# Weight loads in two parts, asked for right behind the split that frees their buffer

## Chip, cores and metric

The kernel runs on one core of one Trainium2 chip. The metric is the device time of one execution in microseconds (us). Before the change it is 750.67 us, the median of three runs (748.7 to 752.8 us).

## What is computed

For each of 1024 samples there are 32 fields of 128 numbers. For each of the 496 pairs of fields (i, j) with i < j there is a weight matrix of 128 x 128. The output of a pair is field i times its matrix, multiplied element by element with field j:

```python
v_i = inputs[:, I_IDX, :]
v_j = inputs[:, J_IDX, :]
transformed = jnp.einsum('bpd,ped->bpe', v_i, W)
return transformed * v_j
```

The output is 1024 x 496 x 128 floats, 260 MB, and has to be written to HBM; the weights are 32.5 MB and the fields 16.8 MB.

## The kernel before

**Pairs and units.** The pairs are taken in the order of falling i: field 30 with 31 first, field 0 with 1 to 31 last. Number q counts pairs (0 to 495); each pair has two units u = 2q and 2q + 1, one for each half of the 1024 samples. The program is one loop over u, in which every engine's instructions are written down in the order in which that engine takes them; nothing is reordered afterwards (`manual_schedule`).

**A unit.** `first(u)` (line 202) issues two matmuls on PE (L212: xh with wh, xl with wl) into one PSUM bank and lets ACT multiply the bank by 1 + 2^-12 (L213). `second`, three units later, issues the third matmul (L221: xd with wd), then DVE multiplies the bank with field j into an output tile (L227). An output tile holds four pairs (2 MB). ACT issues its store (L258). The first 15 pairs use one plain fp32 matmul instead (L209).

**Splits.** Three fast matmuls stand for one exact one, so weights and fields are split into three parts first. `split_w` takes two pairs of weights: ACT makes wh (L127), POOL wl and wd (L128, L129, L130). `split_x` takes half of a field: ACT makes xh (L142), POOL xl (L143, L144), and xd is made by POOL (L148) for fields 0 to 9 and by DVE (L265) for the others. The splits stand in a list `todo`, ordered by the pair that needs them; at the odd units the loop takes one that may start. A split of weights may start five pairs ahead of its use, one of field i at the start of field i + 1's block of pairs.

**Weight loads.** Weights come in 62 chunks of eight pairs (512 KB) into a ring of three buffers (`rpool`). Field 0's load (`x_0`) takes one turn in the same ring, between chunks 54 and 55. A chunk may be loaded once the last of its four splits has read the chunk that had the buffer before. `w_at` says at which pair each load is issued: for chunk c at pair 8c - 17, for chunks 55 to 57 at pair 8c - 11.

**Loads in two parts.** The even chunks from 12 to 60 (`WAPART`, 25 of them) are loaded by `load_apart`: POOL issues 112 rows (448 KB, L102) and SP the other 16 (64 KB, L103). All other chunks are one load of SP (L118). Three pairs behind such a load (`BACK`) POOL issues a tiny DMA into a scratch tile, `move_on` (L99), which moves on the round in which POOL's DMAs take the DMA engines.

**Other loads.** Fields 1 to 16 come in four group loads of 2 MB (`load_group`, L108, tiles x_g), issued by SP at pairs 52, 141, 219 and 313 (`XAT`). Their space holds output tiles until 20 pairs before that, so the number of output buffers falls from seven to three in the course of the run.

**Queues.** POOL takes its splits and its DMA issues in one order; a DMA issue takes its time in that order. SP does nothing but issue loads, in the order of the program, and stands still at one whose buffer is not free yet. ACT's stores stand among its splits and multiplies.

Of the kernel before, what the change touches and what calls it, by code (L numbers as in the profile page):

```python
# [13 lines left out]
NQ = NF * (NF - 1) // 2  # L14
BT = 1024
HB = 512
WC = 2
WL = 8
# [6 lines left out]
WB = 3  # L25
WLEAD = 12
XAFTER = 54
# [3 lines left out]
NE = 14  # L31
ROWS = 8 * NE
WAPART = tuple(range(12, 62, 2))
BACK = 3
# [11 lines left out]
def kernel(  # L46
# [35 lines left out]
    def load_x(f, pieces=1, eng=None):  # L82
        if f == 0:

            t = rpool.tile([P, WL, P], F32, tag="w", name="x_0").rearrange("p q e -> p (q e)")
        else:
            t = xpool.tile([P, BT], F32, tag=f"x{f}", name=f"x_{f}")
        s = BT // pieces
        for k in range(pieces):
            (eng or nc.sync).dma_start(out=t[:, k * s : (k + 1) * s], in_=xt[f, :, k * s : (k + 1) * s])  # L90
        x_sb[f] = t
# [5 lines left out]
    def move_on(k):  # L97

        nc.gpsimd.dma_start(out=mark[: 2 * k], in_=xt[0, : 2 * k, :16].rearrange("(b a) n -> a b n", a=k))  # L99

    def load_apart(dst, src):
        nc.gpsimd.dma_start(out=dst[:ROWS], in_=src[:ROWS].rearrange("(b a) m n -> a b m n", a=NE))  # L102
        nc.sync.dma_start(out=dst[ROWS:], in_=src[ROWS:])  # L103

    def load_group(k):
        t = xpool.tile([P, XG, BT], F32, tag=f"g{k}", name=f"x_g{k}")
        f = XG * k + 1
        nc.sync.dma_start(out=t, in_=xt[f : f + XG].rearrange("m d b -> (m d b)").rearrange("(d m b) -> d m b", m=XG, b=BT))  # L108
        for m in range(XG):
            x_sb[f + m] = t[:, m, :]  # L110

    def load_w(c, splits=(0, WL), eng=nc.sync):
        w_raw[c] = rpool.tile([P, WL, P], F32, tag="w", name=f"w_{c}")
        if c in WAPART:
            load_apart(w_raw[c], wt[c])
            return
        for a, b in zip(splits, splits[1:]):
            eng.dma_start(out=w_raw[c][:, a:b, :], in_=wt[c, :, a:b, :])  # L118

    w_s = {}  # L120

    def split_w(c, u):

        k = c * WC % WL
        raw = w_raw[c * WC // WL][:, k : k + WC, :].rearrange("p q e -> p (q e)")
        h, l, d = [wpool.tile([P, WC * P], F32R, tag=t, name=f"{t}_{c}") for t in ("wh", "wl", "wd")]
        nc.scalar.mul(h, raw, 1.0 - 2.0**-13)  # L127
        nc.gpsimd.tensor_tensor(l, raw, h.bitcast(F32), ALU.subtract)  # L128
        nc.gpsimd.tensor_scalar(d, h.bitcast(F32), EPS, 1.0, ALU.mult, ALU.mult)  # L129
        nc.gpsimd.tensor_tensor(d, l.bitcast(F32), d.bitcast(F32), ALU.subtract)  # L130
        w_s[c] = (h, l, d)

    x_s = {}
    later = []
# [22 lines left out]
    for c in range(c0, nchunk):  # L157
        todo.append(((c - 3) * WC + 1, max(c * WC, nq0), lambda u, c=c: split_w(c, u)))
# [16 lines left out]
    w_at = {}  # L175
    for c in range(WB, -(-NQ // WL)):
        free = (c - WB + 1) * WL if (c - WB) * WL < nq0 else 0
        early = 0 if XAFTER < c <= XAFTER + WB else WLEAD - 6
        w_at[max(c * WL - 3 * WC - 5 - early, free)] = c
    x_at = XAFTER * WL - 11  # L180
    assert x_at not in w_at and len(w_at) == NQ // WL - WB

    w_q = {c: q for q, c in w_at.items()}
    back = []

    ngroup = NF // XG // 2
    group_at = {q: k for k, q in enumerate(XAT)}
# [14 lines left out]
    def first(u):  # L202
        q, h = divmod(u, 2)
        i, c = pairs[q][0], q // WC
        r = slice(q % WC * P, (q % WC + 1) * P)
        s = slice(h * HB, (h + 1) * HB)
        po[u] = ppool.tile([P, HB], F32, tag="po", name=f"po_{u}")
        if q < nq0:
            nc.tensor.matmul(po[u], w_raw[q // WL][:, q % WL, :], x_sb[i][:, s], start=True, stop=True)  # L209
        else:  # L210
            for t in (0, 1):
                nc.tensor.matmul(po[u], w_s[c][t][:, r], x_s[i][t][:, s], start=t == 0, stop=t == 1)  # L212
            nc.scalar.mul(po[u], po[u], 1.0 + EPS)  # L213

    def second(u):
        q, h = divmod(u, 2)
        i, j = pairs[q]
        r = slice(q % WC * P, (q % WC + 1) * P)
        s = slice(h * HB, (h + 1) * HB)
        if q >= nq0:  # L220
            nc.tensor.matmul(  # L221
                po[u], w_s[q // WC][2][:, r], x_s[i][2][:, s], start=False, stop=True, skip_group_check=True
            )
        g, k = divmod(q, OG)
        if k == 0 and h == 0:
            ots[g] = out_tile(g)
        nc.vector.tensor_tensor(ots[g][:, k, s], po.pop(u), x_sb[j][:, s], ALU.mult)  # L227
        if q >= NQ - 2:
            stores.append((u + SLAG, out[g, :, k, s], ots[g][:, k, s]))
        elif g == 0 or q >= NQ - OG:  # L230
            if h == 1:
                stores.append((u + SLAG, out[g, :, k], ots[g][:, k]))
        elif k == OG - 1 and h == 1:
            stores.append((u + SLAG, out[g], ots[g]))

    for u in range(2 * NQ + LAG + SLAG):
        q = u // 2
        if u < 2 * NQ:
            i, j = pairs[q]
            if u % 2 == 0 and j == i + 1 and XG * ngroup < i - 2 - XLEAD:  # L240
                load_x(i - 2 - XLEAD)
            first(u)
            if u == 2 * nq0:
                move_on(5)
            if u % 2 == 0 and q in group_at:
                load_group(group_at[q])
            if u % 2 == 1 and q in w_at:
                load_w(w_at[q])
                if w_at[q] in WAPART:
                    back.append(q + BACK)  # L250
            if u % 2 == 0 and q in back:
                move_on(16 - NE if q < w_q[WAPART[-1]] else 13)
            if u == 2 * x_at + 1:
                load_x(0)
        if LAG <= u < 2 * NQ + LAG:
            second(u - LAG)
        while stores and stores[0][0] <= u - LAG:
            nc.scalar.dma_start(*stores.pop(0)[1:])  # L258
        if u % 2 == 1:
            ready = [t for t in todo if t[0] <= q]  # L260
            if ready:
                ready[0][2](u)
                todo.remove(ready[0])
        while later and later[0][0] <= u:
            nc.vector.tensor_tensor(*later.pop(0)[1:], ALU.subtract)  # L265
    assert not todo and not later and not stores
# [32 lines left out]
```

## Time and profile before

| | |
|---|---|
| time, median of 3 runs | 750.67 us (748.7 to 752.8) |
| the profiled execution | 750.21 us, span 748.4 us |
| PE busy | 699.0 us (93%) |
| DVE busy | 678.0 us (91%) |
| ACT busy | 623.9 us (83%) |
| POOL busy | 611.5 us (82%) |
| moved by DMA | 310.06 MB, mean 414 GB/s |
| loads by POOL (L102) | 25 of 448 KB, 11.8 us to landing |
| stores (L258) | 122 of 2 MB, 13.3 us to landing |

The page gives the busy time of each engine and its share of the span. The chain is the work that ended last, followed back from the end: at each step to what released it. A line with a bracket, such as `[1.16 <-POOL wl L128]`, tells the idle time of the engine just before the instruction and what ended it. A line of waits has the time in all, the number of waits, and the longest. A line of a stretch has its bounds and length, then for each engine the busy time and the number of instructions, then the granted clock of PE (1.00 is full), the busy share of the 16 DMA engines and what they moved. A line of DMA issues has what is moved, the queue, the number, the size of one, and the median time from issue to landing.

### The profile page before, as it was taken

What the parts mean: (1) busy time and instruction counts of PE and PEld (TensorE: products, weight loads), DVE (VectorE), ACT (ScalarE), POOL (GpSimd) and SP (SyncE); (2) the same over time, 40 slices, a digit from 0 to 9 for tenths busy, and PEclk for the clock granted to TensorE, in tenths of its full rate; (3) what the DMA queues carried; (4) which work ended last, traced back from release to release, by engine and by line L of the source; (5) the groups of instructions that cost most, each with busy time, mean ns of one, the idle gap of its engine ahead of it and who ended that gap; (6) DMA issues with size and microseconds to landing.
All of it is one profiled execution on the core that took longest, in us unless ns stands there. A gap on an engine that the chain in (4) does not pass through costs nothing.

```text
span 748.4 us, 11064 instructions
## 1 busy us (share of the span) xinstructions
PE 699.0 (93%) x2946; PEld 556.2 (74%) x2946; DVE 678.0 (91%) x1024; ACT 623.9 (83%) x1256; POOL 611.5 (82%) x902
## 2 busy tenths in 40 slices
PE   7998999999999999979999989899999999989994
PEld 3576778778888877858778777678787787868883
DVE  4999999999999998969989978689899899979994
ACT  1398989889999989968889888689899798969993
POOL 1889999999999988886988878688888889787760
PEclk9999999999999999999999999899999999999998
DMA  9999999999999999999999999999999999999998
GB/s 347 423 427 426 430 427 430 425 425 408 430 428 425 423 421 426 425 423 427 421 432 419 421 421 392 422 409 395 417 414 427 388 391 391 425 401 394 417 428 352
DMA packets 32941, 310.06 MB, mean 414 GB/s; under 512 B 5104, under 2 KB 5232, under 8 KB 16752
## 3 DMA queue, kind: packets, MB, share of 16 engines
q10 hardware_dynamic: 19584, 261.10, 83.0%
q1 hardware_dynamic: 8864, 36.77, 12.3%
q0 software_dynamic: 4432, 11.48, 4.2%
q8 instruction: 24, 0.39, 0.2%
q14 instruction: 37, 0.30, 0.1%
HBM read 49.29 MB, written 260.05 MB: 413 GB/s over the span
## 4 chain that ended last, share of the span: by engine, by line
PE 65%; DMA 14%; POOL 11%; DVE 6%; issue 2%; ACT 0%; DVEq 0%; ACTq 0%; POOLq 0%; SPq 0%
PE po L212 41%; PE po L221 21%; DMA out_dram<-ot 9%; DVE ot L227 6%; PE po L209 4%; DMA x<-in_xt_dram 3%; POOL wl L128 3%; POOL xl L143 2%; POOL wd L130 2%; POOL xd L148 2%; DMA w<-in_wt_dram 1%; POOL xl L144 1%; POOL wd L129 1%; DVE xd L265 1%; ACT po L213 0%
## 5 line engine op out<-in xcount | busy, mean ns | idle before, releaser
L213 ACT ACTIVATE po<-po 128x512 f32<-128x512 f32 x962 | 544.1, 584 | 84.8 <-PE po L212 48.4
L227 DVE TENSOR_TENSOR ot<-po,x 128x512 f32<-128x512 f32 x720 | 473.8, 687 | 36.9 <-DMA out_dram<-ot 17.6
L212 PE MATMUL po<-xl,wl 128*128 128x512 f32 x962 | 380.2, 395 | 19.8 <-POOL wl L128 18.5
L212 PE MATMUL po<-xh,wh 128*128 128x512 f32 x962 | 379.1, 394 | 10.3 <-DVE ot L227 10.3
L221 PE MATMUL po<-xd,wd 128*128 128x512 f32 x962 | 377.9, 393 | 4.2 <-ACT po L213 2.4
L212 PEld LDWEIGHTS po<-xl,wl 128*128 128x128 f32 x962 | 182.5, 190 | 65.4 <-POOL wl L128 25.8
L128 POOL TENSOR_TENSOR wl<-w,wh 128x256 fp32r<-128x256 f32 x241 | 180.3, 748 | 56.5 <-ACT wh L127 51.7
L212 PEld LDWEIGHTS po<-xh,wh 128*128 128x128 f32 x962 | 182.4, 190 | 51.5 <-DVE ot L227 13.2
L221 PEld LDWEIGHTS po<-xd,wd 128*128 128x128 f32 x962 | 182.3, 190 | 44.0 <-issue 3.5
L227 DVE TENSOR_TENSOR ot<-po,x_g 128x512 f32<-128x512 f32 x272 | 179.9, 689 | 24.1 <-PE po L221 18.9
L130 POOL TENSOR_TENSOR wd<-wl,wd 128x256 fp32r<-128x256 f32 x241 | 179.4, 744 | 20.1
L129 POOL TENSOR_SCALAR wd<-wh 128x256 fp32r<-128x256 f32 x241 | 99.1, 411 | 20.6
L127 ACT ACTIVATE wh<-w 128x256 fp32r<-128x256 f32 x241 | 99.4, 413 | 14.0 <-DMA w<-in_wt_dram 8.9
L143 POOL TENSOR_TENSOR xl<-x_g,xh 128x512 fp32r<-128x512 f32 x32 | 41.5, 1296 | 0.1
L144 POOL TENSOR_SCALAR xl<-xl 128x512 fp32r<-128x512 f32 x52 | 36.2, 696 | 4.6
L143 POOL TENSOR_TENSOR xl<-x,xh 128x512 fp32r<-128x512 f32 x20 | 26.3, 1313 | 15.8 <-ACT xh L142 15.5
L209 PE MATMUL po<-x,w 128*128 128x512 f32 x60 | 28.3, 628 | 4.0 <-DMA x<-in_xt_dram 4.0
L265 DVE TENSOR_TENSOR xd<-xh,xl 128x512 fp32r<-128x512 f32 x32 | 29.8, 930 | 0.0
L148 POOL TENSOR_TENSOR xd<-xh,xl 128x512 fp32r<-128x512 f32 x20 | 25.7, 1286 | 1.7
L209 PEld LDWEIGHTS po<-x,w 128*128 128x128 f32 x60 | 11.6, 198 | 19.9 <-issue 12.2
L142 ACT ACTIVATE xh<-x 128x512 fp32r<-128x512 f32 x20 | 12.4, 629 | 11.5 <-DMA x<-in_xt_dram 11.4
L142 ACT ACTIVATE xh<-x_g 128x512 fp32r<-128x512 f32 x32 | 20.2, 631 | 0.0
(7 smaller groups left out, 33.8 us busy)
## 6 DMA issues: line engine op xcount, KB each, us to landing
out_dram<-ot ACTq DMA_DIRECT2D x122, 2048.0 KB, 13.3
w<-in_wt_dram SPq DMA_DIRECT2D x36, 512.0 KB, 11.1
w<-in_wt_dram POOLq DMA_DIRECT2D x25, 448.0 KB, 11.8
x_g<-in_xt_dram SPq DMA_DIRECT2D x4, 2048.0 KB, 20.2
x<-in_xt_dram SPq DMA_DIRECT2D x14, 512.0 KB, 8.9
out_dram<-ot ACTq DMA_DIRECT2D x6, 512.0 KB, 8.6
w<-in_wt_dram SPq DMA_DIRECT2D x26, 64.0 KB, 5.9
x<-in_xt_dram ACTq DMA_DIRECT2D x4, 256.0 KB, 5.9
```

The costliest lines, as they stand in the source:

```text
L127: nc.scalar.mul(h, raw, 1.0 - 2.0**-13)
L128: nc.gpsimd.tensor_tensor(l, raw, h.bitcast(F32), ALU.subtract)
L129: nc.gpsimd.tensor_scalar(d, h.bitcast(F32), EPS, 1.0, ALU.mult, ALU.mult)
L130: nc.gpsimd.tensor_tensor(d, l.bitcast(F32), d.bitcast(F32), ALU.subtract)
L143: nc.gpsimd.tensor_tensor(l, x_sb[f][:, s], h.bitcast(F32), ALU.subtract)
L144: nc.gpsimd.tensor_scalar(l, l.bitcast(F32), 1.0 / EPS, 1.0, ALU.mult, ALU.mult)
L148: nc.gpsimd.tensor_tensor(d, h.bitcast(F32), l.bitcast(F32), ALU.subtract)
L209: nc.tensor.matmul(po[u], w_raw[q // WL][:, q % WL, :], x_sb[i][:, s], start=True, stop=True)
L212: nc.tensor.matmul(po[u], w_s[c][t][:, r], x_s[i][t][:, s], start=t == 0, stop=t == 1)
L213: nc.scalar.mul(po[u], po[u], 1.0 + EPS)
L221: nc.tensor.matmul(po[u], w_s[q // WC][2][:, r], x_s[i][2][:, s], start=False, stop=True, skip_group_check=True)
L227: nc.vector.tensor_tensor(ots[g][:, k, s], po.pop(u), x_sb[j][:, s], ALU.mult)
```

## The change

The loads in two parts are taken out of `w_at`. Instead, `split_w` notes in `spent` each chunk whose last split it has just written down, and at the end of each turn of the loop the next such load (`w_next`) is issued as soon as the chunk that had its buffer is in that list: chunk c - 3, or chunk 54 in the case of chunk 56. For chunk c this is at pair 8c - 23 (or later, where a field's split took that turn) instead of 8c - 17. For chunk 58 it is pair 441, which is ahead of chunk 57's load at pair 445; before, chunk 57 came first. The mark still follows three pairs behind its load.

```diff
-    w_s = {}
+    w_s, spent = {}, []
...
         nc.gpsimd.tensor_tensor(d, l.bitcast(F32), d.bitcast(F32), ALU.subtract)
         w_s[c] = (h, l, d)
+        if (c + 1) * WC % WL == 0:
+            spent.append(c * WC // WL)
...
-        w_at[max(c * WL - 3 * WC - 5 - early, free)] = c
+        if c not in WAPART:
+            w_at[max(c * WL - 3 * WC - 5 - early, free)] = c
...
-    w_q = {c: q for q, c in w_at.items()}
     back = []
+    w_next = list(WAPART)
...
             if u % 2 == 1 and q in w_at:
                 load_w(w_at[q])
-                if w_at[q] in WAPART:
-                    back.append(q + BACK)
             if u % 2 == 0 and q in back:
-                move_on(16 - NE if q < w_q[WAPART[-1]] else 13)
+                move_on(16 - NE if w_next else 13)
...
+        if w_next and (XAFTER if w_next[0] == XAFTER + 2 else w_next[0] - WB) in spent:
+            load_w(w_next.pop(0))
+            back.append(q + BACK)
```

## The prediction

> **What bounds the kernel now.** I read the page first: no engine is the bound all the way (PE 93%, DVE 91%), while the DMA row is full and GB/s sinks from about 427 to about 400 after the middle. So the next views were the engines' busy time by stretch and the waits of each stretch.
>
> ```profile
> core 0: us, PE busy (x) PEld busy (x) DVE busy (x) ACT busy (x) POOL busy (x), PEclk, DMA share, GB/s
> 15.00:282.00 267.00, 258.24 (x1088) 202.87 (x1086) 263.40 (x398) 230.01 (x468) 240.18 (x343) 1.00 1.01 424
> 282.00:345.00 63.00, 57.89 (x243) 46.45 (x244) 52.32 (x83) 52.04 (x107) 52.77 (x79) 0.97 1.01 424
> 345.00:485.00 140.00, 128.94 (x551) 104.35 (x551) 121.76 (x184) 118.06 (x238) 116.97 (x173) 0.98 1.01 419
> 485.00:668.00 183.00, 173.66 (x746) 141.46 (x745) 166.59 (x248) 158.79 (x319) 154.59 (x229) 0.98 1.00 408
> ```
>
> Up to 282 us DVE is full (263.4 of 267) and the DMA engines as well. From 282 to 485 us DVE waits for stores (18.4 us in eight waits), so DMA sets the pace. From 485 us on it hardly does (1.3 us of DVE waits up to 668); there PE and DVE run on the edge and PE loses time in short holes. What makes them is in the timeline of PE and in the chain of waits:
>
> ```profile
> 359.73 0.50 PE L212 MATMUL po<-xl,wl 128*128 128x512 f32 x1 [1.16 <-POOL wl L128]
> 391.77 0.50 PE L212 MATMUL po<-xl,wl 128*128 128x512 f32 x1 [1.82 <-POOL wl L128]
> 503.36 0.50 PE L212 MATMUL po<-xl,wl 128*128 128x512 f32 x1 [1.16 <-POOL wl L128]
> 540.81 0.50 PE L212 MATMUL po<-xl,wl 128*128 128x512 f32 x1 [1.78 <-POOL wl L128]
> ...
> 667.90 0.47 PE L221 MATMUL po<-xd,wd 128*128 128x512 f32 x1 [1.64 <-ACT po L213]
> ```
>
> Each split of a field (two halves of 3.2 us on POOL: L143, L144, L148) makes PE wait once for the weight split behind it. The hole is 1.16 us where nothing else lies in that run (fields 8, 6, 4, 1) and 1.77 to 1.82 us where a POOL DMA issue does (L102, 0.62 us, or L99, 0.63 us: fields 7, 5, 3, 2, 0). The last line is a weight load that comes late:
>
> ```profile
> 655.54 11.15 DMA w<-in_wt_dram
> 667.17 0.59 ACT po L213
> ...
> 666.85 0.42 ACT L127 ACTIVATE wh<-w 128x256 fp32r<-128x256 f32 x1 [6.18 <-DMA w<-in_wt_dram]
> ```
>
> ACT stands 6.18 us before the first split of chunk 56, its multiplies of PSUM (L213) queue behind it, and PE gets a hole of 1.64 us. From there the chain is PE's to 733 us. In all, ACT waits for weights four times, 8.9 us, always on the POOL part:
>
> ```profile
>   ACT wh L127: 8.9, 4
> ```
>
> **What the change does, part by part.** It adds and removes no instruction: 25 loads by POOL (L102) with their 25 marks (L99) and 25 small loads by SP (L103) stand elsewhere. I worked the places out from the order of the program on each engine.
>
> 1. *SP's part.* SP already waits for the last split of the old chunk (L103 behind POOL's L128, 253.8 us in 25 waits), so it leaves when it did before. Only the POOL part (448 KB) comes sooner, by the 5 to 10 us that lie between the two issues now (for example 124.4 and 129.6 us, 648.2 and 655.5 us).
>
> 2. *The late chunk 56: -1.6 us.* Chunk 54's last split ends on POOL at 649.5 us; the load then goes out in POOL's 0.67 us of idle time there, 6.0 us sooner. With its 11.15 us it lands at 660.7 us, and ACT wants it at 666.85 - 6.18 = 660.7 us. The wait goes, and PE's 1.64 us with it. What is late next is POOL: the 1.79 us hole at 662.3 us stays, for the mark now stands directly before field 0's split, where the load had stood between its halves. The other three waits (2.7 us) lie before 380 us, where DMA sets the pace, and count 0 (bounds 0 and -0.75, the largest hole that PE got there).
>
> 3. *POOL's issues against the field splits: 0.* Moved out of the run: fields 7, 5, 3 (1.8 to 1.16 us, -0.6 each). Moved into it: fields 8 and 1 (+0.63 each). Fields 2 and 0 keep one (a mark directly before). After 485 us that is field 3 against field 1, nothing; before, -0.6 us where DMA paces. Bounds -0.6 and +0.6.
>
> 4. *The group load at 463 us: -0.5 us.* DVE waits 5.18 us at 479.28 us for a store that shares the DMA engines with 2 MB of x_g and chunk 40's 448 KB (asked for at 456.3 us). The latter now moves about ten us sooner, and chunk 42 only from 472 us. 448 KB at 428 GB/s are 1.07 us; I take half, as chunk 42 comes into the end of the window. Bounds -1.07 and 0.
>
> 5. *The tail: -0.4 us.* DVE is full from 668 us to the end but for idle times of 1.13 us (707.66) and 0.51 us (713.05). They fall where chunk 60's load (693.0 us) and chunk 61's (697.2 us) run together; now they lie some 10 us apart, as all loads do. The DMA engines are full there too, so I take a quarter of 1.64 us. Bounds -1.64 and 0.
>
> 6. *SP's queue: what else moves.* Chunk 58's small part now stands ahead of chunk 57's load and takes the buffer of x_0, so chunk 57 waits for chunk 55's last split: 664.9 instead of 659.5 us. At 10.4 to 12.7 us of landing it comes at 675.3 to 677.6 us; it was wanted at 676.9 and is now at about 675.3. That is a wait of 0 to 2.3 us on ACT; the wait of 1.80 us at 280.9 us made a hole of 0.75 us on PE, so it costs 0 to 1.0 us: **+0.3**. Two group loads of x also fall behind a small weight load that waits for a split: 204.0 to 212.5 us, and 312.6 to 327.6 us. With 20.7 and 22.7 us to land they come at 233 and 350 us; their first readers on ACT are at 233.4 and 349.1 us. Both are then just in time or a little late, the second by up to some us, since the 7.7 us that DVE lost to stores between 317 and 334 us are partly saved until then. In this stretch a hole of PE is paid out of the stores in flight: 0, bounds 0 and +1.7.
>
> Sum: -1.6 - 0.5 - 0.4 + 0.3 = **-2.2 us**. From the profiled execution's 750.21 us (span 748.4 us and 1.8 us around it; the median of the runs shown is 750.67 us) this makes **748.0 us**.
>
> **A rule against the row.** PE's clock is halved for 3.4 us behind two of the holes and not behind three others of the same length:
>
> ```profile
> 391.80:395.20 3.40, 3.40 (x15) 2.82 (x16) 2.66 (x4) 2.58 (x6) 3.11 (x6) 1.00 1.08 437
> 581.20:584.60 3.40, 3.40 (x9) 2.62 (x9) 1.38 (x2) 1.54 (x3) 3.15 (x6) 0.50 0.96 377
> 663.10:666.50 3.40, 3.16 (x8) 1.95 (x6) 2.04 (x3) 0.00 (x0) 2.90 (x5) 0.50 1.02 414
> ```
>
> Nine matmuls instead of 15 at 0.227 us apiece: 1.4 us each time. The Trainium skill (TensorE: Matmul & The Clock Gate, "Part 1: The HAM clock gate") halves the clock after an idle window of about 3.4 us; by that rule holes of 1.8 us would never be charged and the sum would hold no such term. The rows say otherwise, so every hole of 1.8 us carries a chance of 1.4 us more, two in five. After 485 us the change leaves three of them (fields 2, 1, 0), as before, so the sum gets nothing, the range 1.4 us to either side.
>
> **The rivals.**
> - *Nothing comes of it: 750.2 us.* The DMA engines are full nearly to the end; stores then take back what PE gains at 668 us. For it: the slices from 692 to 730 us move 417 and 428 GB/s. Against: they stand partly idle just then (DMA share 0.96 from 668 us on), and stores land faster to the end.
> - *More comes of it: 745.4 us.* Items 2, 4 and 5 at their far ends (1.64 + 1.07 + 1.64 = 4.35) and one halved clock less (1.4), minus 1.0 for chunk 57: -4.8 us. For it: the loads come evenly, one each eight pairs, instead of 960 KB together.
> - *Slower: 756 us.* After 440 us only three output buffers are left. A tile takes PE 24 matmuls of 0.227 us, 5.44 us, and DVE starts a tile two tiles after it finished the one before in that buffer, 10.9 us; stores land in 9.9 us (median, next lines). An early load takes its 1.07 us from the stores in flight. Where they land at 10.9 us already, each of the nine loads from 485 us on costs DVE that much, and DVE has nothing to spare: up to 9.6 us, say 6. It decides when the median landing rises by 1 us. Against: bytes are the same and come more evenly.
>
> ```profile
> out_dram<-ot ACTq DMA_DIRECT2D x31, 2048.0 KB, 9.9
> w<-in_wt_dram POOLq DMA_DIRECT2D x7, 448.0 KB, 7.7
> ```
>
> - *It does not do what it says* (SP's part cannot come sooner, see 1) concerns an eighth of the bytes; the POOL part does move.
>
> The Trainium skill speaks for the slower case: in DMA: Bandwidth & Descriptors, "Queues, rings and completion order", every DMA engine takes turns between its queues packet by packet, so a load asked for sooner slows the stores of that moment at once. By it alone items 4 and 5 would be 0 and the sum -1.3 us.
>
> **How the numbers follow.** Forecast 748.0 us, chance 0.45; nothing 0.15; more 0.25; slower 0.15. A measurement of this kernel tells about 0.5% from no change, 3.75 us. The forecast and "nothing" lie inside; "more" lies outside, nearly all, and so does the slower case: faster 0.27, same 0.58, slower 0.15. The range reaches from beyond the "more" case (745.4 less one more halved clock, 744.0) up to the bad ends of items 3 and 6 with one halved clock above "nothing" (750.2 + 0.6 + 1.4 + 1.0 = 753.2): **744 to 753.5 us**.
>
> **What would show it.** Right: ACT's 6.18 us at 666.85 us gone; PE holes of 1.8 us at fields 8, 2, 1, 0 and of 1.16 us at 7, 5, 3; the wait at 479 us shorter by up to 1 us; a small wait of ACT at chunk 57. Wrong: stores landing above 10.9 us after 485 us with DVE waiting for them, or ACT waiting several us for x_g at about 345 us and the DMA share sinking behind it.

## The result, and the profile after

The changed kernel takes **750.88 us** (median of 12 runs, 748.38 to 754.07), the kernel before 750.15 us beside it (12 runs, 747.92 to 754.43). The ratio is 1.0012 with a 95% interval of 0.9992 to 1.0032: no difference that can be told. The profiled execution took 751.54 us, with a span of 749.8 us. New line numbers: the first two matmuls of a unit are L215, ACT's multiply L216, the third matmul L224, DVE's multiply L230, xl L145, xd by DVE L269; the weight splits (L127 to L130) and the issues (L99, L102, L103, L118) keep theirs.

The stretches of the changed kernel, columns as before:

```profile
15.00:282.00 267.00, 257.99 (x1079) 202.15 (x1078) 260.87 (x395) 229.33 (x466) 241.78 (x342) 0.99 1.01 423
282.00:345.00 63.00, 60.32 (x262) 48.47 (x261) 54.77 (x86) 55.54 (x114) 54.61 (x82) 1.00 1.01 423
345.00:485.00 140.00, 126.86 (x535) 102.38 (x534) 115.60 (x180) 115.83 (x232) 116.36 (x173) 0.97 0.99 413
485.00:668.00 183.00, 175.32 (x750) 142.96 (x749) 168.20 (x252) 160.77 (x322) 152.06 (x225) 0.98 1.00 409
```

Up to 282 us, where DVE had been full (263.4 us), DVE now does less (260.9 us, 395 instructions against 398), with PE's clock at 0.99 instead of 1.00: something is lost in a stretch of which the prediction's sum says nothing. The next row has it back (86 instructions against 83), the third falls behind again (180 against 184), and the fourth makes that up (252 against 248). At 668 us both kernels stand at 913. So these rows show where the two differ, but not which of the differences lasts.

The late side first: PE's holes in the timeline, at the splits of fields 3, 1 and 0.

```profile
543.94 0.50 PE L215 MATMUL po<-xl,wl 128*128 128x512 f32 x1 [1.16 <-POOL wl L128]
...
625.90 0.50 PE L215 MATMUL po<-xl,wl 128*128 128x512 f32 x1 [1.78 <-POOL wl L128]
666.06 0.50 PE L215 MATMUL po<-xl,wl 128*128 128x512 f32 x1 [1.78 <-POOL wl L128]
```

ACT's timeline at the first split of chunk 56:

```profile
664.36 0.41 ACT L127 ACTIVATE wh<-w 128x256 fp32r<-128x256 f32 x1
```

The stores issued between 485 and 668 us, with their median landing:

```profile
out_dram<-ot ACTq DMA_DIRECT2D x31, 2048.0 KB, 9.7
```

The bracket at ACT's split of chunk 56 is gone, and with it PE's 1.64 us. The holes are 1.15 to 1.16 us at fields 7 to 3 and 1.78 to 1.79 us at fields 2, 1 and 0, as forecast. Stores land in 9.7 us (9.9 before), so the slower rival's condition is not met.

The early side: DVE's waits between 113 and 255 us, a stretch in which it waits for no store in either kernel. Before:

```profile
DVE ot L227 <- PE po L221: 0.3, 1, 0.3
```

After:

```profile
DVE ot L230 <- PE po L224: 3.0, 4, 1.4
```

And the DVE time of the 14 subtractions that make xd in that stretch (bounds, length, busy time and number, clock, DMA share, GB/s). Before:

```profile
113.00:255.00 142.00, 12.46 (x14) 1.00 1.01 424
```

After:

```profile
113.00:255.00 142.00, 13.92 (x14) 0.99 1.01 421
```

DVE waits for PE 2.7 us longer (and 0.2 us for POOL), and its 14 subtractions take 1.5 us more. Why, the timeline of POOL and DVE at the split of one field (14) shows. Before:

```profile
195.66 1.29 POOL L143 TENSOR_TENSOR xl<-x_g,xh 128x512 fp32r<-128x512 f32 x1
196.78 0.73 DVE L265 TENSOR_TENSOR xd<-xh,xl 128x512 fp32r<-128x512 f32 x1
...
200.05 0.62 POOL L102 DMA_DIRECT2D w<-in_wt_dram  x1
...
204.71 0.63 POOL L99 DMA_DIRECT2D mark<-in_xt_dram  x1
```

After:

```profile
192.87 0.62 POOL L102 DMA_DIRECT2D w<-in_wt_dram  x1
193.52 1.31 POOL L145 TENSOR_TENSOR xl<-x_g,xh 128x512 fp32r<-128x512 f32 x1
...
197.61 0.63 POOL L99 DMA_DIRECT2D mark<-in_xt_dram  x1
198.27 1.31 POOL L145 TENSOR_TENSOR xl<-x_g,xh 128x512 fp32r<-128x512 f32 x1
198.89 1.24 DVE L269 TENSOR_TENSOR xd<-xh,xl 128x512 fp32r<-128x512 f32 x1
```

Before, both issues stood behind the two halves of the split. Now the load stands directly ahead of the first half and the mark between the halves. POOL's second half comes later, and DVE's subtraction for the first half, which is placed by the pair count, now meets it and takes 1.24 us instead of 0.73. It is the same at fields 15, 13 and 12; at fields 16 and 11 the mark alone stands directly ahead of the first half.

### The profile page after: what moved, and what is told of

It is laid out like the page before. It is cut to its first block, busy times and chain, and to the rows that moved or that the text cites. A ratio compares the mean times of both kernels' runs of the same rounds, so it can differ in the third digit from the quotient of the medians.

```text
span 749.8 us, 11063 instructions
## 1 busy us (share of the span) xinstructions
PE 703.2 (94%) x2946; PEld 558.8 (75%) x2946; DVE 675.3 (90%) x1024; ACT 626.8 (84%) x1256; POOL 613.6 (82%) x902
## 4 chain that ended last, share of the span: by engine, by line
PE 69%; DMA 15%; POOL 8%; DVE 4%; issue 2%; ACT 1%; DVEq 0%; ACTq 0%; POOLq 0%; SPq 0%
PE po L215 44%; PE po L224 22%; DMA out_dram<-ot 12%; DVE ot L230 4%; PE po L212 4%; DMA x<-in_xt_dram 3%; POOL wl L128 2%; POOL xl L145 1%; POOL xd L150 1%; POOL wd L130 1%; POOL xl L146 1%; DVE xd L269 1%; POOL wd L129 1%; ACT po L216 0%; POOL w L102 0%
## 5 line engine op out<-in xcount | busy, mean ns | idle before, releaser
L216 ACT ACTIVATE po<-po 128x512 f32<-128x512 f32 x962 | 546.2, 583 | 92.9 <-PE po L215 55.4
L230 DVE TENSOR_TENSOR ot<-po,x 128x512 f32<-128x512 f32 x720 | 470.4, 686 | 43.4 <-DMA out_dram<-ot 22.3
L215 PE MATMUL po<-xl,wl 128*128 128x512 f32 x962 | 381.1, 396 | 19.5 <-POOL wl L128 18.0
L215 PE MATMUL po<-xh,wh 128*128 128x512 f32 x962 | 380.3, 395 | 11.3 <-DVE ot L230 11.1
L224 PE MATMUL po<-xd,wd 128*128 128x512 f32 x962 | 378.9, 394 | 1.8 <-DVE xd L269 0.9
L215 PEld LDWEIGHTS po<-xl,wl 128*128 128x128 f32 x962 | 183.2, 190 | 66.4 <-POOL wl L128 26.4
L128 POOL TENSOR_TENSOR wl<-w,wh 128x256 fp32r<-128x256 f32 x241 | 183.2, 760 | 53.5 <-ACT wh L127 48.9
L215 PEld LDWEIGHTS po<-xh,wh 128*128 128x128 f32 x962 | 183.2, 190 | 52.9 <-DVE ot L230 14.2
L224 PEld LDWEIGHTS po<-xd,wd 128*128 128x128 f32 x962 | 183.1, 190 | 41.3 <-ACT po L216 2.4
L230 DVE TENSOR_TENSOR ot<-po,x_g 128x512 f32<-128x512 f32 x272 | 179.5, 689 | 22.1 <-PE po L224 14.4
L130 POOL TENSOR_TENSOR wd<-wl,wd 128x256 fp32r<-128x256 f32 x241 | 179.0, 743 | 20.1
L127 ACT ACTIVATE wh<-w 128x256 fp32r<-128x256 f32 x241 | 99.2, 412 | 5.1 <-DVE ot L230 3.0
L145 POOL TENSOR_TENSOR xl<-x_g,xh 128x512 fp32r<-128x512 f32 x32 | 41.6, 1299 | 3.4 <-ACT xh L144 3.0
L145 POOL TENSOR_TENSOR xl<-x,xh 128x512 fp32r<-128x512 f32 x20 | 26.3, 1314 | 15.6 <-ACT xh L144 15.3
L269 DVE TENSOR_TENSOR xd<-xh,xl 128x512 fp32r<-128x512 f32 x32 | 31.0, 970 | 0.2 <-POOL xl L146 0.2
L212 PEld LDWEIGHTS po<-x,w 128*128 128x128 f32 x60 | 11.8, 202 | 19.7 <-issue 12.4
L144 ACT ACTIVATE xh<-x 128x512 fp32r<-128x512 f32 x20 | 12.4, 628 | 11.2 <-DMA x<-in_xt_dram 11.1
```

The costliest lines, as they stand in the source:

```text
L145: nc.gpsimd.tensor_tensor(l, x_sb[f][:, s], h.bitcast(F32), ALU.subtract)
L224: nc.tensor.matmul(po[u], w_s[q // WC][2][:, r], x_s[i][2][:, s], start=False, stop=True, skip_group_check=True)
```

## The experiments

Each is told by its ratio to the kernel before, timed beside it; 0.001 is 0.75 us. "Sooner" means asked for as in the change; chunks that are not sooner stand at before's places. **Stretch** is the time from store 19 to store 44 (about 114 to 255 us) in the profile.

| kernel | sooner | ratio (95%) | stretch, us |
|---|---|---|---|
| before | none | 1 | 140.3 |
| e1_only56 | 56 | 0.9961 (0.9936 to 0.9985) | 140.3 |
| e2_late | 42 to 60 | 0.9970 (0.9945 to 0.9996) | 140.5 |
| e3_early | 12 to 40 | 1.0041 (1.0021 to 1.0060) | 144.1 |
| e4_clear | all, issues put off | 0.9984 (0.9961 to 1.0007) | 140.9 |
| e5_half_a | 12 to 26, 42 to 60 | 1.0005 (0.9986 to 1.0025) | 143.9 |
| e6_half_b | 28 to 60 | 0.9987 (0.9965 to 1.0010) | 140.3 |
| e7_clear_old | 56, issues put off | 1.0329 (1.0291 to 1.0367) | 147.1 |
| after | all | 1.0012 (0.9992 to 1.0032) | 143.9 |
| e8_after_again | all | 1.0002 (0.9978 to 1.0026) | 143.7 |
| e9_no12 | 14 to 60 | 1.0024 (0.9992 to 1.0055) | 143.3 |
| e10_add12 | 12, 42 to 60 | 0.9974 (0.9955 to 0.9994) | 141.5 |
| e11_late_clear | 42 to 56, issues put off | 0.9966 (0.9942 to 0.9990) | 140.6 |
| e12_clear_early | all, issues of 12 to 40 put off | 0.9957 (0.9926 to 0.9987) | 140.8 |

A single profile is one execution out of a spread of 6 to 10 us: the two profiles of the changed kernel have spans of 749.8 and 746.6 us. So the end of a profile proves nothing here at this size; what counts is the timed ratio, and what comes again in every profile.

The theory at the outset: chunk 56's gain is real and is given back by the early loads, mostly where the output buffers fall from four to three at 440 to 460 us (DVE waits 5.39 us at 443 us in the changed kernel). The rivals: DMA paces the whole, so that places do not matter; or the halved clock decides by chance.

A correction to some expectations: they call the field whose split makes PE's hole at 141 us field 13. Counted back from field 0 it is **field 17**.

**Late against early.** The edit of e1, against the changed kernel (e2 and e3 differ in the tuple alone):

```diff
+SOONER = (56,)
...
-        if c not in WAPART:
+        if c not in SOONER:
...
-    w_next = list(WAPART)
+    w_next = list(SOONER)
...
                 load_w(w_at[q])
+                if w_at[q] in WAPART:
+                    back[q + BACK] = w_at[q]
```

> Before's places for all POOL weight loads, but chunk 56 alone is asked for right behind chunk 54's last split. Theory (the gain at chunk 56 is real, and in the change it is given back elsewhere): ACT's 6.18 us wait ahead of the first split of chunk 56 is gone, PE's hole of 1.64 us behind it too, nothing before 640 us moves; time 1.6 us below before (748.5 against 750.1). Rival (DMA bound to the end: stores take back what PE gains): the wait goes, but the time stays at before's, within 0.5 us, and DVE's waits for stores behind 668 us grow by about 1.6 us.

> The change for chunks 42 to 60 alone; chunks 12 to 40 keep before's places. Theory: everything up to about 440 us is as in before, the loss at 440 to 460 us is small since chunk 40's load is not sooner, and chunk 56's 1.6 us are gained: 748 to 748.5 us, against before -1.6 to -2. Rival (a sooner load costs the stores beside it its 1.07 us wherever three output buffers are left): +3 to +6 us against before, stores landing above 10.5 us behind 485 us. Rival (when a load is asked for does not matter): as before, within 0.5 us.

> The change for chunks 12 to 40 alone; from chunk 42 on before's places, so chunk 56 comes late again. Theory (the change loses early what it gains late): the PE hole of 2 us at about 141 us and DVE's wait of over 5 us at about 443 us are there as in after, and ACT's 6.2 us wait at chunk 56 too; +2 to +3 us against before, so 752 to 753 us. Rival (the loss at 440 to 460 us is made by chunk 42 and the later loads): 750 us, as before. Rival (what is lost up to 460 us is a toss of the halved clock and not of the loads): as before, within 0.5 us on the median, with the losses in one profile and not in another.

Measured: 0.9961, 0.9970 and 1.0041. Chunk 56 alone gives 2.9 us (1.1 to 4.8), the 1.6 us within it. The other nine late chunks add nothing that can be told. The early chunks alone cost 3.1 us (1.6 to 4.5), and in that kernel the late wait is back (ACT, first split of chunk 56):

```profile
670.43 0.42 ACT L128 ACTIVATE wh<-w 128x256 fp32r<-128x256 f32 x1 [5.88 <-DMA w<-in_wt_dram]
```

So "no difference" is a gain and a loss of one size. "Places do not matter" falls: all three kernels differ from before by more than their interval, the third in the other direction.

**POOL's issues out of the field splits.** e4: loads and marks are put off until the run of splits is over; the turns of the splits are worked out beforehand.

```diff
+    no_load = {q for a, b in xs.values() for q in range(a - 1, b + 1)}
+    no_mark = {q for a, b in xs.values() for q in range(a, b + 2)}
...
-            load_w(w_next.pop(0))
-            back.append(q + BACK)
+            due.append(w_next.pop(0))
+        if u % 2 == 1 and due and not back and q not in no_load:
+            back[q + BACK] = due[0]
+            load_w(due.pop(0))
```

> The change, but POOL's load and mark are put off until the run of field splits in which they would fall is over (and a mark is not put directly ahead of one), so that no field split has a POOL issue in its run. Theory (POOL's issue of 0.6 us between two field splits lengthens PE's hole from 1.16 to 1.8 us and brings the halved clock with it): all holes are 1.16 us, the one of 2.0 us at 141 us is gone, no halved clock behind 500 us; 2 to 5 us below after, 746 to 749 us. Rival (the halved clock comes anyway, behind holes of 1.16 us too): 0.6 us for each of three fields, so 1.8 us below after at the most. Rival (DMA paces to the end): within 0.5 us of after, and DVE's waits for stores take up what PE gains.

Measured: 0.9984, which is 1.2 us below before with an interval that takes in no change, and 2.1 us below the changed kernel's 1.0012. No hole of 1.8 us is left at a field's split behind 380 us. The hole at 141 us stays (1.99 us), for another reason than an issue in that run. And a new wait came, at chunk 57, in ACT's timeline:

```profile
678.24 0.42 ACT L128 ACTIVATE wh<-w 128x256 fp32r<-128x256 f32 x1 [3.27 <-DMA w<-in_wt_dram]
```

PE's timeline just behind it:

```profile
679.28 0.47 PE L237 MATMUL po<-xd,wd 128*128 128x512 f32 x1 [2.22 <-ACT po L229]
```

That is the prediction's step 6. Over the nine profiles in which chunk 58's small part stands ahead of chunk 57's load, that load landed in 4.6 to 7.0 us six times, with no wait; in 10.7 to 13.6 us three times (e4, e5, e10), with waits of 3.27, 3.35 and 1.47 us on ACT and holes of 2.22, 2.29 and 0.42 us on PE.

**Which early loads.** e5 and e6 part the early chunks (the tuple of e5, against e2's; e6 has chunks 28 to 60); e7 puts the issues off without asking sooner, but for chunk 56 (the tuple of e1 with the edit of e4).

```diff
-SOONER = (42, 44, 46, 48, 50, 52, 54, 56, 58, 60)
+SOONER = (12, 14, 16, 18, 20, 22, 24, 26, 42, 44, 46, 48, 50, 52, 54, 56, 58, 60)
```

> The change for chunks 12 to 26 and 42 to 60; chunks 28 to 40 keep before's places. It parts the 3 to 4 us that the early loads cost (chunks 12 to 40 alone: 1.0041 of before; chunks 42 to 60 alone: 0.997; all: 1.0012). Theory (the loss comes where stores lack buffers, at 440 to 460 us, so from chunks 28 to 40): 0.998 of before, about 749.5 us, with the PE hole of 2 us at 141 us costing 0.7 us and DVE's wait at 440 us under 3.5 us. Rival (the loss is made early: POOL's mark between field 13's splits at 141 us with the halved clock behind it, and three holes of 0.3 us): 1.0005 to 1.002 of before, 751.5 to 752.5 us.

> The change for chunks 28 to 40 and 42 to 60; chunks 12 to 26 keep before's places: the counterpart of the run before. Theory (buffer drop): 1.000 to 1.001 of before, 751 us, with DVE waiting 5 us for a store at about 443 us. Rival (the loss is made before 282 us): 0.997 to 0.998, 749 us. If both halves lie at 0.999, the loss is spread over all early loads and neither place makes it.

> Before's places for all POOL weight loads but chunk 56's, which is asked for sooner, and POOL's loads and marks put off until no field split has one in its run. Theory: the 2.9 us that chunk 56 alone gave, and 0.6 us for each of three fields behind 485 us that had holes of 1.8 us (fields 3, 2, 0), and most of their halved clocks (1.4 us each, two in five): 745.5 to 747.5 us, 0.992 to 0.9945 of before. Rival (a POOL issue put off makes a weight load late again, 3 us of ACT's wait): 0.996, as with chunk 56 alone. Rival (DMA paces here): holes of 1.16 us, but no time gained over chunk 56 alone, 0.996.

Measured: 1.0005, 0.9987, 1.0329. Against chunks 42 to 60 alone, the first half (12 to 26) costs 2.6 us, the second 1.3 us; the two intervals overlap, but the stretch is long in the first and short in the second. **The theory of the buffer drop falls**: DVE's wait at about 443 us comes in kernels of both kinds, whether the load there is sooner or not. DVE's timeline in the changed kernel's second profile:

```profile
443.46 4.88 DVE L230 TENSOR_TENSOR ot<-po,x 128x512 f32<-128x512 f32 x8 [5.49 <-DMA out_dram<-ot]
```

And in e10, where no chunk from 14 to 40 is sooner:

```profile
444.69 4.28 DVE L231 TENSOR_TENSOR ot<-po,x 128x512 f32<-128x512 f32 x7 [4.86 <-DMA out_dram<-ot]
```

In that stretch DMA paces, and a wait that grows in one place is missing in another: at 482 us the first of these two waits 4.89 us, the second 1.54. Added up over 430 to 500 us, DVE's idle times of over 0.25 us are 13.7 us before, 14.1 and 14.4 in the two profiles of the changed kernel, 15.0 in e2 and 13.6 in e10.

e7 shows what asking sooner is worth as slack: at before's places there is none, and an issue that is put off makes its load late, here by 10 us on ACT.

```profile
500.77 0.42 ACT L128 ACTIVATE wh<-w 128x256 fp32r<-128x256 f32 x1 [10.23 <-DMA w<-in_wt_dram]
```

**One hole, or the whole stretch.** The next suspect was the hole of 2.0 us at 141 us, with a halved clock behind it. e9 leaves chunk 12 alone at before's place, e10 moves it alone among the early ones to the new place, e8 is the changed kernel again. e11 puts off the issues of chunks 42 to 56 and leaves all others where they were.

The tuple of e10, against e2's; e9 has chunks 14 to 60, e11 chunks 42 to 56 with e4's edit for these alone.

```diff
-SOONER = (42, 44, 46, 48, 50, 52, 54, 56, 58, 60)
+SOONER = (12, 42, 44, 46, 48, 50, 52, 54, 56, 58, 60)
```

> The changed kernel once more, beside the runs that follow, to see which of its stalls come again. Theory (the holes are set by the order of the instructions, so they come again; the halved clocks do not all): PE's hole of 2.0 us at 141 us, three of 0.3 us at 201, 224 and 246 us, 1.16 us at fields 7 to 3 and 1.8 us at fields 2 to 0; 1.001 of before. The waits of DVE for stores at 443 and 482 us, 10.6 us together, may lie elsewhere but come to 8 to 13 us between 430 and 500 us. Rival (the two traces of before and after differ by chance): the hole at 141 us is 1.35 us this time.

> The change for all but chunk 12, whose load and mark keep before's places (129.6 and 136 us instead of 125.6 and 128 us). Theory (the early loss is one place: chunk 12's issues moved out of field 13's run leave a hole of 2.0 us there with a halved clock behind it, 2.5 us in a stretch where DVE is full): hole 1.35 us, no halved clock at 141 us, 2 us less than after, so 0.998 to 0.9985 of before. Rival (the early loss is spread over all early loads, by DMA): as after, 1.001, with stores some 2 us behind before's all the same by 282 us.

> The change for chunk 12 and for chunks 42 to 60; chunks 14 to 40 keep before's places: the counterpart of the run before. Theory (one place): the hole of 2.0 us and the halved clock at 141 us are there, 2 us above chunks 42 to 60 alone (0.997), so 0.9995 of before. Rival (spread over all early loads): 0.997, as without chunk 12. Rival (the hole comes, but DMA takes it up again by 345 us): 0.997 with the hole in the trace.

> Chunks 42 to 56 asked for sooner, and of these alone POOL's loads and marks put off until no field split has one in its run; all other loads at before's places, so that chunk 57's load does not stand behind chunk 58's small part. Theory: all of the gain of chunks 42 to 60 alone (0.997) and 0.6 us for each of three fields behind 485 us, with most of two halved clocks: 0.993 to 0.9955, 746 us, no hole over 1.2 us behind 485 us but those from stores. Rival (DMA takes up what PE gains here): 0.997, with DVE's waits for stores behind 485 us 3 to 5 us longer than where the holes are 1.8 us. Rival (loads put off come late): above 1, with ACT waiting for weights.

Measured: 1.0002, 1.0024, 0.9974, 0.9966. **That theory falls too.** The hole follows chunk 12 (2.03 us in e8, 1.96 in e10, 1.38 in e9), but the time does not: without the hole e9 is no faster, and with it e10 is as fast as chunks 42 to 60 alone. The two DVE rows of 113 to 255 us show what makes the stretch long or short. The waits of e9:

```profile
DVE ot L231 <- PE po L225: 0.6, 2, 0.3
```

Its subtractions:

```profile
113.00:255.00 142.00, 15.03 (x14) 1.00 1.01 420
```

The waits of e10:

```profile
DVE ot L231 <- PE po L225: 3.0, 4, 1.4
```

Its subtractions:

```profile
113.00:255.00 142.00, 11.81 (x14) 0.99 1.00 415
```

In e9 DVE idles next to nothing, yet its subtractions take 2.6 us more than before: the stretch is 3.0 us longer. In e10 DVE idles 2.7 us more, but its subtractions take 0.6 us less, and the stretch grows by 1.2 us only (the two do not add up exactly, since DVE's instructions overlap a little in the trace). Most of the longer stretch belongs to chunks 14 to 26, at fields 16 to 12.

e11 took every hole of 1.8 us behind 500 us away (field 0's is shown; at fields 2 and 1 at most 1.19 us are left) and is not measurably faster than e1 or e2:

```profile
661.99 0.50 PE L228 MATMUL po<-xl,wl 128*128 128x512 f32 x1 [1.18 <-POOL wl L129]
```

The 1.8 us that three such holes should bring are within the interval (1.8 us to either side), and DVE waits 2.4 us for stores from 485 to 668 us (2.2 in e1, 6.1 in e2), so the rival that DMA takes them up has nothing for it. What these holes are worth stays open.

**The early issues put off.** e12 is the changed kernel with e4's edit for chunks 12 to 40 alone.

```diff
+    due, put_off = [], range(12, 42)
...
+        if due and (due[0] not in put_off or u % 2 == 1 and not back and q not in no_load):
```

> The change for all chunks, but for chunks 12 to 40 POOL's load and mark are put off until no field split has one in its run; chunks 42 to 60 as in the change. Theory (the early loads cost 3 us up to 282 us because the change puts POOL's load and mark into the field splits of that stretch: PE's holes there and DVE's subtraction for xd, which takes 1.2 to 1.9 us where it meets POOL's subtraction for xl, 0.7 to 0.85 us otherwise): between stores 19 and 44, 140.5 to 141.5 us instead of 143.3 to 144.1 us, and 0.997 of before like chunks 42 to 60 alone, 748 us; with chunk 57's wait of 2.2 us for its weights, if it comes as in the kernel with all issues put off, 0.9985. Rival (the early loads cost by what they take from the stores, not by POOL's order): 1.001 as the change, with that stretch short or not.

Measured: 0.9957, 3.2 us below before and 3.4 to 4.1 us below the changed kernel's two ratios. The stretch is 140.8 us. DVE's waits in it are before's again but for the hole at 141 us:

```profile
DVE ot L243 <- PE po L237: 1.4, 1, 1.4
```

Its subtractions are at before's 12.4 us:

```profile
113.00:255.00 142.00, 12.37 (x14) 1.00 1.01 420
```

One reservation: put off past fields 15 to 12, these loads go out at 180.6, 202.5, 224.4 and 246.3 us. This trace is 2.0 us behind before's at store 19, so that is nearly where they stood before (178.2, 200.1, 221.9, 243.8), and e12 alone does not tell POOL's order from the time of the transfer. Within the stretch they can be told apart: DVE waits for no store in it, in any of these kernels, so a transfer that takes DMA from the stores cannot have cost anything there. Behind it they cannot.

All kernels together: where chunks 14 to 26 are sooner and not put off, the stretch is 143.3 to 144.1 us and the ratio 1.0002 to 1.0041 (five kernels). Elsewhere it is 140.3 to 141.5 us and the ratio 0.9957 to 0.9987 (seven; e7, whose loads come late, left out). The four of the five that also have chunk 56 sooner lie at 1.0011 on the mean, the seven at 0.9971: 3.0 us apart, and their stretches are 3.0 us apart on the mean as well (143.7 and 140.7). e1, e2, e10, e11 and e12 lie below before by 0.3 to 0.4%, each by more than its interval; among them nothing can be told. The rival of the halved clock does not explain the difference between e2 or e12 and the changed kernel: the mean granted clock of the twelve runs is 0.984 in all of them, both timings of the changed kernel included. In e1 (0.986) and e11 (0.988) it is higher than in the kernel before beside them (0.984 and 0.985), so there it may have a part.

But the long stretch is not shown to be the lost time. From store 44 to store 74 (254 to 432 us in before), where DMA paces, the five kernels with the long stretch need 173.7 to 175.4 us and the eight others, before among them, 176.5 to 179.3 us. From store 19 to store 74 the means are then 318.6 and 318.2 us: the traces have the loss back. From store 74 to the last store it is 306.8 to 311.8 us against 304.0 to 310.5 us, which single profiles cannot tell apart. So the early loads cost about 3 us of time (e3) and nothing that can be told where their issues are put off (e12), but at which place in the run the 3 us arise stays open.

## Why the prediction was right, and where it was wrong

Forecast 748.0 us, measured 750.88: inside the range, and inside "no change that can be told". But not by the forecast's path. Against the kernel before, timed beside it, the change is +0.9 us (-0.6 to +2.4), which leaves out the forecast's -2.2. That the range held is its width, and some luck: its main late step came out, and a cost of the early loads that is not in its sum cancelled it.

- *Step 1 (SP's part cannot come sooner):* right, by the order of the program.
- *Step 2 (chunk 56, -1.6 us):* right. The load went out at 653.2 us and landed at 661.34 us, ahead of ACT's split at 664.36 us; all ACT waits for loads in two parts are gone. Alone it measures -2.9 us (-4.8 to -1.1).
- *Step 3 (POOL's issues against the field splits: 0, bounds -0.6 and +0.6):* **this is the step that failed.** Its holes behind 380 us came exactly as listed. But it listed fields 8 to 0 only, and gave no reason why the earlier ones should cost nothing. Up to 282 us the first fence of the prediction itself shows DVE full, and there the change moves both issues of four loads into the splits of fields 15 to 12, and the marks of two more directly ahead of fields 16 and 11. None of the rivals has this. What the runs showed in its place: the stretch from store 19 to store 44 is 3.0 to 3.8 us longer wherever these issues stand so, and the early loads cost 3.1 us of time (e3), five times the bound, and nothing that can be told where their issues are put off (e12). That the first of these makes the second was argued and is not shown, since the traces have the stretch's loss back by 432 us.
- *Step 4 (group load at 463 us, -0.5 us):* wrong, nothing came. The wait is 5.19 and 4.89 us against 5.18, and the sum of the waits around it is the same. So in these two profiles the wait does not go by the one load beside it (chunk 40's, asked for at 451.4 us instead of 456.3); that it goes by what DMA has to move in all is the reading that is left, and was not tested.
- *Step 5 (tail, -0.4 us):* in the direction, not told by time. DVE's two idle times of 1.13 and 0.51 us became 0.58 and 0.32 us (0.80 and 0.33 in the second profile).
- *Step 6 (chunk 57, +0.3 us):* the mean was about right, the bounds too narrow: nothing in both profiles of the changed kernel, but 0.4 to 2.3 us of PE in three of nine profiles with that order; (2.22 + 2.29 + 0.42) / 9 is 0.55 us. The second x_g load came late as forecast (asked for at 331.65 us, landed at 350.71): ACT waits 0.25 us for it. PE's hole beside it (2.80 us at 348.40 us) is put down to DVE, which waits 4.72 us there for a store, and not to x_g.
- *The halved clock (two in five of the holes of 1.8 us):* over 14 profiles, holes of 1.7 to 2.1 us were followed by a halved clock 21 times in 50. Which of them is mostly a matter of where the hole lies in time (last section), and less of chance.
- *The rivals:* "nothing comes of it" has the nearest time, 750.2 us, but its mechanism (stores take back what PE gains) is not what happened: chunk 56's gain stays where it stands alone. The slower case needed stores landing in over 10.9 us; they land in 9.7.

What stays open: where in the run the early loads cost their 3 us, and by what, since the part that is lost up to 255 us is back by 432 us; and why the hole at field 17 is 2.0 us with chunk 12 sooner though its issues then lie ahead of that run. That POOL's order and not the transfers' time lengthens the stretch rests on the rows of the stretch, not on a kernel that moves one without the other; for the time of the whole, the two are not told apart.

## What to carry to other kernels

A change that moves many like instructions has to be priced in every stage, first in the one whose engine is full; a list of the places that begins where the waiting begins leaves out the stage without waits, in which a moved instruction is paid at once. Whether such a payment reaches the end is a second question: here the stage behind, paced by DMA, gave it back in every trace. When such a change measures as nothing, its two halves may be a gain and a loss: time them apart before concluding that it does nothing. And a DMA issue in the order of a compute engine (POOL here) is an instruction of 0.6 us like any other: ask for a load early enough that its issue can be put where that engine has nothing urgent.

## What the runs showed of the hardware

**DVE and POOL do not run two such subtractions side by side.** In the pairs shown here and above, DVE's xd (both inputs in SBUF; 0.68 us where it meets none) ends 0.55 us after the POOL subtraction that it meets, however long that makes it. Two more pairs, at field 15. Before:

```profile
173.79 1.29 POOL L143 TENSOR_TENSOR xl<-x_g,xh 128x512 fp32r<-128x512 f32 x1
174.49 1.15 DVE L265 TENSOR_TENSOR xd<-xh,xl 128x512 fp32r<-128x512 f32 x1
```

After:

```profile
175.85 1.92 DVE L269 TENSOR_TENSOR xd<-xh,xl 128x512 fp32r<-128x512 f32 x1
175.92 1.30 POOL L145 TENSOR_TENSOR xl<-x_g,xh 128x512 fp32r<-128x512 f32 x1
```

POOL ends at 175.08 and DVE at 175.64 us; POOL at 177.22 and DVE at 177.77. At field 14 it is 196.95 and 197.51 before, 199.58 and 200.13 after. The Trainium skill (SBUF — State Buffer, "Who interferes with whom") says that a DVE instruction with two SBUF inputs contends with a GpSimd instruction that reads SBUF, and that the order of issue decides which of the two is blocked. The rows agree, but in the last pair POOL's subtraction starts 0.07 us behind DVE's in the trace and it is DVE that waits. Where DVE is further ahead it is POOL that waits: in e9, at field 16, DVE starts 0.67 us sooner and POOL takes 1.75 us instead of 1.30.

```profile
155.73 1.26 DVE L272 TENSOR_TENSOR xd<-xh,xl 128x512 fp32r<-128x512 f32 x1
156.40 1.75 POOL L146 TENSOR_TENSOR xl<-x_g,xh 128x512 fp32r<-128x512 f32 x1
```

**The clock is halved behind some holes of 1.8 us, and behind none of under 1.7.** PE's holes between 60 and 700 us in 14 profiles, with how many were followed by 3.4 us (or twice that) at half clock:

| hole, us | in all | halved |
|---|---|---|
| 0.6 to 1.7 | 183 | 0 |
| 1.7 to 2.1 | 50 | 21 |
| 2.1 to 3.0 | 20 | 16 |
| over 3.0 | 22 | 22 |

The clock records in the 14 traces show which. All 73 halved stretches begin a whole number of steps of 3.413 us (to within 0.002 us) behind the first entry of their record. Between 60 and 700 us there are 2,474 such steps at full clock with less than 1.75 us of idle PE in them, and none was followed by a halved one; of 45 with over 1.85 us all were, and of the 19 between them 14. So a hole of 1.8 us is mostly charged when it lies whole within one step, and else goes free: of the 50 holes of 1.7 to 2.1 us, 24 do, and 19 of these were followed by a halved clock; of the 26 that a step's end divides, two were, both about 2 us long.

One of them in the changed kernel, behind the hole at 141 us:

```profile
141.40:144.80 3.40, 3.40 (x10) 2.61 (x8) 2.00 (x3) 1.73 (x3) 3.21 (x5) 0.50 1.02 434
```

A hole of 1.2 us sets PE back by its own length; one of 1.8 us by its own length and, two times in five, by about 1.4 us more. So 0.6 us on the wrong side of 1.7 us sets PE back, on the mean, by about twice as much; what of that reaches the end was not shown (e11).
